# Attention heads on one core: squares, zero tests, row products and gate products move off VectorE

## The chip, the cores and the metric

The kernel runs on one core of a Trainium2 chip. The metric is the device time of one execution in microseconds, the median of three runs. The core's engines are TensorE (PE in the profile, its weight loads PEld), VectorE (DVE), ScalarE (ACT), GpSimd (POOL) and SyncE (SP), which only issues DMAs. All arithmetic that matters here is in float32.

## The reference

Two layers work on 3327 rows of 256 features, padded by the kernel to 3328, 26 tiles of 128 rows. Layer 0 is a graph layer and a mixture of eight experts; layer 1 is a graph attention layer and a block of attention heads. The change is in the last block alone, `_L1_ffn_ref`, which takes the normalized rows `x` and whose result is added to the rows:

```python
sx = einsum('bsh,ndh->bnsd', x, hl_w) + hl_b          # 4 heads n of 64 features d
pad = sx == 0
q = einsum('bnsd,neod->bneso', sx, wq)                # 4 queries e per head
k = einsum('bnsd,nod->bnso', sx, wk);  v = einsum('bnsd,nod->bnso', sx, wv)
att = softmax(einsum('bnesd,bntd->bnest', q, k) * d ** 0.5 + causal)
qkv = where(pad, 0.0, einsum('bnest,bntd->bnesd', att, v))
gs = softmax(einsum('bnsf,nef->bnse', out, gate_w) + gate_b)   # out: qkv with e and d side by side
mixed = sum over e of qkv * gs
hn = layernorm(mixed + sx, ln_g, ln_b)                # over the 64 features of each head, eps 1e-8
hx = relu(where(fx == 0, 0, fx @ fc1 + b1))           # fx: hn with the heads side by side
hx = layernorm(where(fx == 0, 0, hx @ fc2 + b2) + fx, fnorm_g, fnorm_b)
fg = softmax(fout @ fgate_w.T)                        # 4 gates, one per head
result = fout * fg
```

## The kernel before

`graph0`, `Experts.run` and `graph1` do the first three blocks in the first 985 us or so; `heads` does the last one and takes the rest. In `heads` every engine's instructions run in the order in which the Python code issues them: the helper `InOrder` ties each instruction to the one before it on the same engine, which is why the profile shows almost everything at line 61, and why groups are told apart by the names of their tiles.

The work of `heads` is cut into units, one for each tile `t` of 128 rows and each head `h`, and a unit into chunks of up to 512 earlier columns (`span`): a unit of tile `t` has `t // 4 + 1` chunks, 392 in all. For each chunk there is

- `fill` (TensorE): scores of four queries into four PSUM tiles `pqk`; the last chunk of a unit gets the causal mask by products with `own` and `after`;
- `drain` (VectorE): each of the four is copied to the SBUF tile `sc` and its row maximum taken; after the last chunk of a unit the maxima become `nmax` (`anmax` in the profile);
- `weigh` (ScalarE): four exponentials in place, with their sums in `den` (each followed by an accumulator read);
- `values` (SP's queue): four DMAs that bring the values `vr` from HBM;
- `turn` (VectorE): one transposition of `sc` in 32x32 blocks;
- `attend` (TensorE): products of `vr` and `sc`, added up in `po`.

At the end of a unit `over` copies `po` to `ot` (ScalarE) and multiplies it by `sxd`, which holds 1 where `sx` is not 0 (GpSimd); one iteration later `back` turns it through TensorE (`ptO`) and copies `qkv` and the gate products `glp` out. The loop over the chunks, with `k` the chunk of `attend`, issues drains a few chunks ahead (`wanted`), `attend(k)`, `turn(k + 1)`, values and half of the exponentials of chunk `k + 2`, `back`, `over`, one step of each open tail and preparation, the other half of the exponentials, and at most one `fill`. From tile 8 on the step of tails and preparations is left out in the iteration after a unit's end:

```python
if not ended or u["t"] < 8:
    run(tails)
    run(preps)
```

Two kinds of generators are stepped there, one step (up to the next `yield`) per iteration:

- `prepare(t)`, for the tile after the current one: a DMA brings `xres`; statistics (`pst`, `pmv`, `prs`); the normalized row `xn`; its transposition `xt`; `psxt` and from it `sxt`; four DMAs on SP's queue spread it to `sxd`, `v`, the keys `kt`, the queries `qt`; last `sxd` is compared with 0 and `sx` turned.
- `tail(t)`, once the four heads of a tile are there: the gates `gs` by `softmax4`, the mixture in `qkv` and `fx`, `norm4(fx)` (tiles `l1..`), the two linear layers (`ph`, `h`, `fo`), `norm4(fo)` (tiles `l2..`), the gates `fg` by `softmax4`, the last products and the DMA to the output. Up to three tails are open; `back` steps them until at most two are left before it adds one.

Copies out of PSUM that either engine can do go through `empty`, which keeps estimates of the work of ScalarE and VectorE in `load` and gives each copy to the engine that would be done first. It decides while the program is built. Each `load[...] +=` line of the diff below therefore also moves the copies that follow.

Of the kernel before, what the change touches and what calls it, by code (L numbers as in the profile page):

```python
# [12 lines left out]
F32 = mybir.dt.float32  # L13
# [13 lines left out]
D = 256  # L27
# [74 lines left out]
class Net:  # L102
# [670 lines left out]
    def heads(self, xs, vs, out):  # L773
        tc, a = self.tc, self.a
        nc = InOrder(tc)
        Q = 32
        with ExitStack() as ctx:
            one = ctx.enter_context(tc.tile_pool(name="at", bufs=1))
# [4 lines left out]
            sm = ctx.enter_context(tc.tile_pool(name="atsm", bufs=4))  # L783
# [7 lines left out]
            lng = self.load_rows(one, a["lng"][:64], 64, "lng")  # L791
            lnb = self.load_rows(one, a["lnb"][:64], 64, "lnb")
# [4 lines left out]
            fng = self.load_rows(one, a["fng"][:64], 64, "fng")  # L797
# [9 lines left out]
            for s in range(2):  # L807
                r = ds(64 * s, 64)
                for k in range(2):
# [3 lines left out]
                    for c in range(2):  # L813
                        self.nc.sync.dma_start(
                            out=wq[r, c, :, ts(k, 64)],
# [54 lines left out]
            def turned(src, dst):  # L870
# [3 lines left out]
                    nc.tensor.transpose(pt[:, k, :], src[:, ts(k, P)], self.ident)  # L874
                empty(dst, pt, D)

            def prepare(t, res):  # L880

                x = tl.tile([P, D], F32, tag="xres", name="xres", bufs=2)
                nc.sync.dma_start(out=x, in_=xs[ts(t, P), :])
                yield
                st = sm.tile([P, 6], F32, tag="pst", name="pst")
                mv = sm.tile([P, 2], F32, tag="pmv", name="pmv")
                rs = sm.tile([P, 1], F32, tag="prs", name="prs")
                nc.vector.bn_stats(st, x)
                nc.vector.bn_aggr(mv, st)
                nc.vector.tensor_scalar(rs, mv[:, 1:2], 1e-5, None, ALU.add)  # L890
                nc.gpsimd.tensor_tensor(rs, rs, self.nhalf[:, :1], ALU.pow)
                load["dve"] += 0.7
                yield
                xn = self.work.tile([P, D], F32, tag="xn", name="xn2", bufs=1)
                nc.vector.tensor_scalar(xn, x, mv[:, 0:1], rs, ALU.subtract, ALU.mult)
                load["dve"] += 0.35
                yield
                xt = self.work.tile([P, 2, P], F32, tag="xt", name="xt2")
                turned(xn, xt)
                yield  # L900
                pp = ps.tile([P, 2, P], F32, tag="b", name="psxt")
                for c in range(2):
                    for k in range(2):
                        nc.tensor.matmul(
                            pp[:, c, :], hlt[:, k, ts(c, P)], xt[:, k, :], start=(k == 0), stop=(k == 1)
                        )
                sxt = self.work.tile([P, 2, P], F32, tag="sxt", name="sxt")
                for c in range(2):
                    nc.scalar.activation(
                        sxt[:, c, :], pp[:, c, :], AF.Identity, bias=hlb[:, c : c + 1]  # L910
                    )
                load["act"] += 0.6
                yield

                sxd = self.work.tile([P, 4, P], F32, tag="sxd", name="sxd", bufs=3)
                for k in range(2):
                    for s in range(2):
                        nc.sync.dma_start(
                            out=sxd[ds(64 * k, 64), s::2, :], in_=sxt[ds(64 * s, 64), :, :]
                        )  # L920
                pp = ps.tile([P, 4, 64], F32, tag="b", name="pv")
                for c in range(2):
                    nc.tensor.matmul(
                        pp[:, 2 * c : 2 * c + 2, :], sxt[:, c, :], wv[:, c, :], start=True, stop=True
                    )
                v = self.work.tile([P, 4, 64], F32, tag="v", name="v", bufs=1)
                empty(v, pp, D)
                yield

                pp = [ps.tile([P, 2, P], F32, tag="b", name="pk") for _ in range(2)]  # L930
                for c in range(2):
                    for s in range(2):
# [12 lines left out]
                qt = tl.tile([P, 4, 2, P], F32, tag="qt", name="qt")  # L945
                pp = [ps.tile([P, 2, 2, P], F32, tag="b", name="pq") for _ in range(2)]
                for c in range(2):
                    for i in range(2):
                        for s in range(2):
                            r = ds(64 * s, 64)  # L950
                            nc.tensor.matmul(
                                pp[s][:, c, i, :], wq[r, c, i, :], sxt[r, c, :], start=True, stop=True
                            )

                for s in range(2):
                    empty(qt[:, s::2, :, :], pp[s], BLK, 8.0)
                yield
                nc.vector.tensor_scalar(sxd, sxd, 0.0, None, ALU.not_equal)
                load["dve"] += 0.4
                sx = tl.tile([P, D], F32, tag="sx", name="sx", bufs=5)  # L960
                turned(sxt.rearrange("p c q -> p (c q)"), sx.rearrange("p (c q) -> p c q", c=2))
                res.update(sx=sx, sxd=sxd, qt=qt)
# [80 lines left out]
            def turn(u, g):  # L1043
# [4 lines left out]
                nc.vector.transpose(w, w)  # L1048
                load["dve"] += 0.1 + 0.00417 * n


            po = ps_o.tile([P, 4, BLK], F32, tag="po", name="po")
            po = po[:, :, :P].rearrange("p q (e i) -> p q e i", e=4)
# [55 lines left out]
            def softmax4(g, n, tag):  # L1109

                g3 = g.rearrange("p (n e) -> p n e", e=4)
                m = sm.tile([P, n], F32, tag=tag + "m", name=tag + "m")
                s = sm.tile([P, 4 * n], F32, tag=tag + "s", name=tag + "s")
                s3 = s.rearrange("p (n e) -> p n e", e=4)
                nc.vector.tensor_reduce(m, g3, AX.X, ALU.max)
                nc.vector.tensor_tensor(s3, g3, m.unsqueeze(2).to_broadcast([P, n, 4]), ALU.subtract)
                yield
                nc.scalar.activation(s, s, AF.Exp)
                yield
                nc.vector.tensor_reduce(m, s3, AX.X, ALU.add)  # L1120
                nc.vector.reciprocal(m, m)
                nc.vector.tensor_tensor(s3, s3, m.unsqueeze(2).to_broadcast([P, n, 4]), ALU.mult)
                load["dve"] += 0.6
                load["act"] += 0.25
                return s

            def norm4(v, g, b, tag):

                mv = sm.tile([P, 4, 2], F32, tag=tag + "mv", name=tag + "mv")
                for h in range(4):  # L1130
                    st = sm.tile([P, 6], F32, tag=tag + "st", name=tag + "st")
                    nc.vector.bn_stats(st, v[:, ts(h, 64)])
                    nc.vector.bn_aggr(mv[:, h, :], st)
                rs = sm.tile([P, 4], F32, tag=tag + "rs", name=tag + "rs")
                nc.vector.tensor_scalar(
                    rs, mv.rearrange("p h s -> p s h")[:, 1, :], 1e-8, None, ALU.add
                )
                load["dve"] += 1.1
                nc.gpsimd.tensor_tensor(rs, rs, self.nhalf[:, :4], ALU.pow)
                v3 = v.rearrange("p (h d) -> p h d", h=4)  # L1140
                nc.gpsimd.tensor_tensor(v3, v3, mv[:, :, 0:1].to_broadcast([P, 4, 64]), ALU.subtract)
                nc.gpsimd.tensor_tensor(v3, v3, rs.unsqueeze(2).to_broadcast([P, 4, 64]), ALU.mult)
                nc.gpsimd.tensor_tensor(v3, v3, rows(g), ALU.mult)
                nc.gpsimd.tensor_tensor(v3, v3, rows(b), ALU.add)

            def tail(t, sx, qkv, glp, den):
# [13 lines left out]
                nc.vector.tensor_tensor(gl, gl, gb, ALU.add)  # L1160
                load["dve"] += 0.9
                gs = yield from softmax4(gl, 4, "gs")
                nc.vector.tensor_tensor(gs, gs, rd, ALU.mult)
                mx = qkv.rearrange("p h e d -> p (h e) d")
                nc.gpsimd.tensor_tensor(
                    mx, mx, gs.unsqueeze(2).to_broadcast([P, 16, 64]), ALU.mult
# [7 lines left out]
                nc.gpsimd.tensor_tensor(fx, fx, sx, ALU.add)  # L1174
                yield
                yield
                norm4(fx, lng, lnb, "l1")
                yield
                yield
                fxt = tl.tile([P, 2, P], F32, tag="fxt", name="fxt", bufs=2)  # L1180
# [22 lines left out]
                nc.gpsimd.tensor_tensor(fo, fo, fx, ALU.add)  # L1203
                yield
                yield
                norm4(fo, fng, fnb, "l2")
                yield
                yield
                fot = tl.tile([P, 2, P], F32, tag="fxt", name="fot", bufs=2)
# [640 lines left out]
```

## Time and profile before

| | |
|---|---|
| median of 3 runs | 3073.84 us (3071.78 to 3076.59) |
| the profiled execution | 3072.57 us, of which the span from first to last instruction 3070.9 us |
| mean TensorE clock granted | 0.965 |
| busy in the span: PE / DVE / ACT / POOL | 2704.3 / 2496.3 / 1676.9 / 888.8 us |
| VectorE: emptying `pqk` to `sc` | 1568 instructions, 897.6 us busy |
| VectorE: turning `sc` | 392 instructions, 816.0 us busy |
| ScalarE: exponentials in `sc`, with reads of their sums | 1568 pairs, 1041.2 and 302.9 us busy |
| GpSimd: `ot` times `sxd` | 104 instructions, 132.7 us busy |

An engine's busy time is the time in which at least one of its instructions runs; neighbouring instructions of an engine overlap a little, so the sum of durations is more than the time they take. A wait names the instruction whose end released the waiting one. The chain is found by going back from the last instruction, at each step to what released it, or to the instruction ahead of it on its engine.

### The profile page before, as it was taken

Reading aid. Unit: us, or ns where it says so; the run is one execution under the profiler, and the core shown is the slowest. Engines: PE = TensorE matmul, PEld = TensorE weight load, DVE = VectorE, ACT = ScalarE, POOL = GpSimd, SP = SyncE. Lnnn points to the kernel's source line nnn. Section 1 sums busy time; section 2 is a strip of 40 time slices with the busy share of each in tenths; the row PEclk is TensorE's granted clock in tenths of the full one; section 3 lists DMA queues with packets and bytes.
Section 4 is the critical chain, followed back from the end, with each engine's and each line's share of the span. In section 5 each row is a group of like instructions: output and inputs, shape, how many; then the busy total and the mean of one; then the engine's idle time right before and its main releaser. Section 6 shows DMA issues by size and latency. Waiting matters only on the chain.

```text
span 3070.9 us, 126719 instructions
## 1 busy us (share of the span) xinstructions
PE 2704.3 (88%) x54254; PEld 2009.7 (65%) x54254; DVE 2496.3 (81%) x6166; ACT 1676.9 (55%) x4566; POOL 888.8 (29%) x1208
## 2 busy tenths in 40 slices
PE   7999988788887888998999998899989999999884
PEld 5878878666776666666666666666656665666553
DVE  5103643799996678999999999999999999999994
ACT  6410145555553546666666665666656666565663
POOL 6431644711223254432232221222111211111112
PEclk9999999999998889999999999999999999999997
DMA  9994578566763223333333343333333333333431
GB/s 375 356 301 137 185 242 265 182 240 230 262 235 95 66 69 90 109 93 99 110 103 102 111 115 102 103 108 111 108 105 109 111 112 112 111 108 108 118 108 52
DMA packets 258193, 449.80 MB, mean 146 GB/s; under 512 B 58816, under 2 KB 156608, under 8 KB 257504
## 3 DMA queue, kind: packets, MB, share of 16 engines
q1 hardware_dynamic: 241232, 416.77, 44.3%
q0 software_dynamic: 6576, 18.02, 1.6%
q8 instruction: 428, 7.01, 1.0%
q10 hardware_dynamic: 9824, 6.91, 0.8%
q14 instruction: 133, 1.09, 0.1%
HBM read 393.37 MB, written 25.88 MB: 137 GB/s over the span
## 4 chain that ended last, share of the span: by engine, by line
DVE 44%; PE 21%; issue 3%; POOL 2%; ACT 1%; DMA 1%; SPq 0%; ACTq 0%; DVEq 0%; POOLq 0%
DVE sc L61 37%; PE po L61 7%; PE pqk L61 7%; PE acc L61 2%; PE ptO L61 2%; DVE l2mv L61 1%; PE pq L61 1%; DVE l1mv L61 1%; PE psxt L61 1%; DVE fo L61 0%; ACT sc L61 0%; DVE l2st L61 0%; DVE anmax L61 0%; DMA vr<-vs 0%; PE ph L61 0%
## 5 line engine op out<-in xcount | busy, mean ns | idle before, releaser
L61 ACT ACTIVATE sc<-sc,anmax 128x512 f32<-128x512 f32 (+3 forms) x1568 | 1041.2, 671 | 122.5 <-DVE anmax L61 122.3
L61 DVE TENSOR_SCALAR_CACHE_REDUCE sc<-pqk 128x512 f32<-128x512 f32 (+3 forms) x1568 | 897.6, 626 | 51.3 <-PE pqk L61 49.2
L61 PEld LDWEIGHTS po<-sc,vr 32*64 32x64 f32 x43728 | 667.6, 132 | 338.4 <-DVE sc L61 190.5
L61 PE MATMUL po<-sc,vr 32*64 32x128 f32 x43728 | 770.3, 277 | 120.9 <-DVE sc L61 70.4
L61 PE MATMUL pqk<-kt,qt 64*128 64x512 f32 (+3 forms) x3136 | 794.8, 579 | 42.5 <-DVE sc L61 16.9
L61 DVE STREAM_TRANSPOSE sc<-sc 128x2048 f32<-128x2048 f32 (+3 forms) x392 | 816.0, 2082 | 9.3 <-ACT sc L61 9.2
L61 PEld LDWEIGHTS pqk<-kt,qt 64*128 64x128 f32 x3136 | 312.5, 186 | 229.5 <-issue 80.5
L61 PE MATMUL acc<-wh,p 128*128 128x259 f32 x1352 | 309.9, 387 | 33.9 <-DVE p L61 33.9
L61 POOL TENSOR_TENSOR ot<-ot,sxd 128x512 f32<-128x512 f32 x104 | 132.7, 1276 | 658.3 <-ACT ot L61 628.5
L61 PEld LDWEIGHTS acc<-wh,p 128*128 128x128 f32 x1352 | 254.1, 190 | 92.1 <-DVE p L61 51.7
L61 PE MATMUL acc<-y,pan 128*128 128x256 f32 x1352 | 304.1, 385 | 11.1 <-DMA pan<-in_adjt_dram 9.4
L61 ACT ACTIVATION_READ_ACCUMULATOR sc<-sc,anmax 128x1 f32 x1568 | 302.9, 193 | 0.0
L61 PEld LDWEIGHTS acc<-y,pan 128*128 128x128 f32 x1352 | 258.3, 193 | 52.7 <-issue 17.1
L61 ACT ACTIVATE u<-u,d 128x512 f32<-128x512 f32 (+1 forms) x182 | 125.2, 688 | 158.7 <-DVE u L61 158.5
L61 ACT COPY qkv<-ptO 128x256 f32<-128x256 f32 x104 | 38.7, 372 | 226.4 <-PE ptO L61 226.4
L61 DVE SCALAR_TENSOR_TENSOR u<-bc,d 128x512 f32<-128x512 f32 (+1 forms) x182 | 135.3, 744 | 0.1
L61 PE MATMUL ptO<-igw,ot 128*128 128x68 f32 x832 | 116.7, 284 | 20.4 <-DVE sc L61 10.3
L61 DVE SCALAR_TENSOR_TENSOR p<-pan,u 128x512 f32<-128x512 f32 (+1 forms) x182 | 126.0, 692 | 10.6 <-PE acc L61 5.8
L61 PEld LDWEIGHTS ptO<-igw,ot 128*128 128x128 f32 x832 | 102.4, 194 | 39.5 <-issue 19.9
L61 DVE DVE_READ_ACCUMULATOR sc<-pqk 128x1 f32 x1568 | 128.2, 82 | 0.0
L61 ACT ACTIVATE junk<-ar 128x1664 bf16<-128x1664 f32 x52 | 82.7, 1591 | 65.3 <-DMA ar<-in_adj_dram 64.1
L61 PEld LDWEIGHTS <-own 64*128 64x128 bf16 x832 | 53.4, 94 | 92.9 <-issue 80.4
(286 smaller groups left out, 2868.0 us busy)
## 6 DMA issues: line engine op xcount, KB each, us to landing
vr<-vs SPq DMA_DIRECT2D x976, 128.0 KB
ar<-in_adj_dram SPq DMA_DIRECT2D x104, 832.0 KB
vr<-vs SPq DMA_DIRECT2D x544, 96.0 KB
pan<-in_adjt_dram SPq DMA_DIRECT2D x156, 256.0 KB
pan<-in_adjt_dram SPq DMA_DIRECT2D x26, 1024.0 KB
pan<-in_adjt_dram SPq DMA_DIRECT2D x20, 832.0 KB
w1e<-w SPq DMA_DIRECT2D x59, 256.0 KB
took<-places SPq DMA_DIRECT2D x59, 129.0 KB
```

What stands on the lines that cost most here:

```text
L61: made = make(*args, **kw)
```

## The change

It touches `heads` alone.

- **`norm4`**: instead of `bn_stats` and `bn_aggr` for each of four heads and an addition on VectorE, there is one sum over all four heads on VectorE (with the sign turned, `ns`), and four Square operations on ScalarE with the sum as bias, a scale of 64, and their sums in `rs`. GpSimd then scales `ns` and `rs` and goes on with power, shift and products as before. Two yields are new, so a norm takes three iterations instead of one.
- **`prepare`**: the normalized row `xn` is made by two GpSimd operations instead of one on VectorE, and the power before it is moved behind the yield, into the same step.
- **comparison with 0**: a new function `nonzero` takes Sign and then Square on ScalarE of the 256 columns of `sxt` into `nz`, and the four DMAs spread `nz` to `sxd`. The comparison of the 512 columns of `sxd` on VectorE is gone.
- **gates**: the last product of `softmax4` and the product of `gs` with `rd` are made by GpSimd.
- the estimates in `load` change with these.

```diff
@@ -874,6 +874,12 @@
                     nc.tensor.transpose(pt[:, k, :], src[:, ts(k, P)], self.ident)
                 empty(dst, pt, D)
+            def nonzero(dst, src):
+                nc.scalar.activation(dst, src, AF.Sign)
+                nc.scalar.activation(dst, dst, AF.Square)
+                load["act"] += 0.75
@@ -888,12 +894,12 @@
                 nc.vector.bn_stats(st, x)
                 nc.vector.bn_aggr(mv, st)
                 nc.vector.tensor_scalar(rs, mv[:, 1:2], 1e-5, None, ALU.add)
+                load["dve"] += 0.7
+                yield
                 nc.gpsimd.tensor_tensor(rs, rs, self.nhalf[:, :1], ALU.pow)
-                load["dve"] += 0.7
-                yield
                 xn = self.work.tile([P, D], F32, tag="xn", name="xn2", bufs=1)
-                nc.vector.tensor_scalar(xn, x, mv[:, 0:1], rs, ALU.subtract, ALU.mult)
-                load["dve"] += 0.35
+                nc.gpsimd.tensor_tensor(xn, x, mv[:, 0:1].to_broadcast([P, D]), ALU.subtract)
+                nc.gpsimd.tensor_tensor(xn, xn, rs.to_broadcast([P, D]), ALU.mult)
                 yield
                 xt = self.work.tile([P, 2, P], F32, tag="xt", name="xt2")
                 turned(xn, xt)
@@ -909,6 +915,8 @@
                     nc.scalar.activation(
                         sxt[:, c, :], pp[:, c, :], AF.Identity, bias=hlb[:, c : c + 1]
                     )
+                nz = self.work.tile([P, 2, P], F32, tag="nz", name="nz", bufs=1)
+                nonzero(nz, sxt)
                 load["act"] += 0.6
                 yield
@@ -916,7 +924,7 @@
                 for k in range(2):
                     for s in range(2):
                         nc.sync.dma_start(
-                            out=sxd[ds(64 * k, 64), s::2, :], in_=sxt[ds(64 * s, 64), :, :]
+                            out=sxd[ds(64 * k, 64), s::2, :], in_=nz[ds(64 * s, 64), :, :]
                         )
                 pp = ps.tile([P, 4, 64], F32, tag="b", name="pv")
                 for c in range(2):
@@ -955,8 +963,6 @@
                 for s in range(2):
                     empty(qt[:, s::2, :, :], pp[s], BLK, 8.0)
                 yield
-                nc.vector.tensor_scalar(sxd, sxd, 0.0, None, ALU.not_equal)
-                load["dve"] += 0.4
                 sx = tl.tile([P, D], F32, tag="sx", name="sx", bufs=5)
                 turned(sxt.rearrange("p c q -> p (c q)"), sx.rearrange("p (c q) -> p c q", c=2))
                 res.update(sx=sx, sxd=sxd, qt=qt)
@@ -1048,6 +1054,8 @@
                 nc.vector.transpose(w, w)
                 load["dve"] += 0.1 + 0.00417 * n
+            sq = one.tile([P, 64], F32, name="sq")
             po = ps_o.tile([P, 4, BLK], F32, tag="po", name="po")
             po = po[:, :, :P].rearrange("p q (e i) -> p q e i", e=4)
@@ -1119,26 +1127,31 @@
                 yield
                 nc.vector.tensor_reduce(m, s3, AX.X, ALU.add)
                 nc.vector.reciprocal(m, m)
-                nc.vector.tensor_tensor(s3, s3, m.unsqueeze(2).to_broadcast([P, n, 4]), ALU.mult)
-                load["dve"] += 0.6
+                nc.gpsimd.tensor_tensor(s3, s3, m.unsqueeze(2).to_broadcast([P, n, 4]), ALU.mult)
+                load["dve"] += 0.4
                 load["act"] += 0.25
                 return s
             def norm4(v, g, b, tag):
-                mv = sm.tile([P, 4, 2], F32, tag=tag + "mv", name=tag + "mv")
+                v3 = v.rearrange("p (h d) -> p h d", h=4)
+                ns = sm.tile([P, 4], F32, tag=tag + "ns", name=tag + "ns")
+                nc.vector.tensor_reduce(ns, v3, AX.X, ALU.add, negate=True)
+                load["dve"] += 0.35
+                yield
+                rs = sm.tile([P, 4], F32, tag=tag + "rs", name=tag + "rs")
                 for h in range(4):
-                    st = sm.tile([P, 6], F32, tag=tag + "st", name=tag + "st")
-                    nc.vector.bn_stats(st, v[:, ts(h, 64)])
-                    nc.vector.bn_aggr(mv[:, h, :], st)
-                rs = sm.tile([P, 4], F32, tag=tag + "rs", name=tag + "rs")
-                nc.vector.tensor_scalar(
-                    rs, mv.rearrange("p h s -> p s h")[:, 1, :], 1e-8, None, ALU.add
-                )
-                load["dve"] += 1.1
+                    nc.scalar.activation(
+                        sq, v[:, ts(h, 64)], AF.Square, bias=ns[:, h : h + 1], scale=64.0,
+                        accum_out=rs[:, h : h + 1],
+                    )
+                load["act"] += 1.2
+                yield
+                nc.gpsimd.tensor_scalar(ns, ns, 1 / 64, None, ALU.mult)
+                nc.gpsimd.tensor_scalar(rs, rs, 1 / 64**3, 1e-8, ALU.mult, ALU.add)
                 nc.gpsimd.tensor_tensor(rs, rs, self.nhalf[:, :4], ALU.pow)
-                v3 = v.rearrange("p (h d) -> p h d", h=4)
-                nc.gpsimd.tensor_tensor(v3, v3, mv[:, :, 0:1].to_broadcast([P, 4, 64]), ALU.subtract)
+                nc.gpsimd.tensor_tensor(v3, v3, ns.unsqueeze(2).to_broadcast([P, 4, 64]), ALU.add)
                 nc.gpsimd.tensor_tensor(v3, v3, rs.unsqueeze(2).to_broadcast([P, 4, 64]), ALU.mult)
                 nc.gpsimd.tensor_tensor(v3, v3, rows(g), ALU.mult)
                 nc.gpsimd.tensor_tensor(v3, v3, rows(b), ALU.add)
@@ -1160,7 +1173,7 @@
                 nc.vector.tensor_tensor(gl, gl, gb, ALU.add)
                 load["dve"] += 0.9
                 gs = yield from softmax4(gl, 4, "gs")
-                nc.vector.tensor_tensor(gs, gs, rd, ALU.mult)
+                nc.gpsimd.tensor_tensor(gs, gs, rd, ALU.mult)
                 mx = qkv.rearrange("p h e d -> p (h e) d")
                 nc.gpsimd.tensor_tensor(
                     mx, mx, gs.unsqueeze(2).to_broadcast([P, 16, 64]), ALU.mult
@@ -1174,7 +1187,7 @@
                 nc.gpsimd.tensor_tensor(fx, fx, sx, ALU.add)
                 yield
                 yield
-                norm4(fx, lng, lnb, "l1")
+                yield from norm4(fx, lng, lnb, "l1")
                 yield
                 yield
                 fxt = tl.tile([P, 2, P], F32, tag="fxt", name="fxt", bufs=2)
@@ -1203,7 +1216,7 @@
                 nc.gpsimd.tensor_tensor(fo, fo, fx, ALU.add)
                 yield
                 yield
-                norm4(fo, fng, fnb, "l2")
+                yield from norm4(fo, fng, fnb, "l2")
                 yield
                 yield
                 fot = tl.tile([P, 2, P], F32, tag="fxt", name="fot", bufs=2)
```

More of the change, by code (lines that the diff above doesn't have):

```diff
@@ L890, in prepare @@
                 nc.vector.tensor_scalar(rs, mv[:, 1:2], 1e-5, None, ALU.add)
-                nc.gpsimd.tensor_tensor(rs, rs, self.nhalf[:, :1], ALU.pow)
                 load["dve"] += 0.7
                 yield
+                nc.gpsimd.tensor_tensor(rs, rs, self.nhalf[:, :1], ALU.pow)
                 xn = self.work.tile([P, D], F32, tag="xn", name="xn2", bufs=1)
-                nc.vector.tensor_scalar(xn, x, mv[:, 0:1], rs, ALU.subtract, ALU.mult)
-                load["dve"] += 0.35
+                nc.gpsimd.tensor_tensor(xn, x, mv[:, 0:1].to_broadcast([P, D]), ALU.subtract)
+                nc.gpsimd.tensor_tensor(xn, xn, rs.to_broadcast([P, D]), ALU.mult)
                 yield
```

## The prediction, as put on record before the run

> **What bounds the kernel now.** I read the page's busy times first, then the stretches in order of time, the chain that ended last, and only then the groups, because a busy share over the whole span mixes stages. `heads` runs from about 985 us to the end. Busy times per engine (part 1 of the page), then three rows of the stretches (us; PE, PEld, DVE, ACT, POOL busy; clock; DMA):
>
> ```profile
> PE 2704.3 (88%) x54254; PEld 2009.7 (65%) x54254; DVE 2496.3 (81%) x6166; ACT 1676.9 (55%) x4566; POOL 888.8 (29%) x1208
> ```
>
> ```profile
> 985.00:1200.00 215.00, 171.62 (x3019) 132.99 (x3021) 145.63 (x489) 108.90 (x372) 87.37 (x100) 0.83 0.28 72
> 1200.00:3000.00 1800.00, 1639.00 (x45950) 1120.25 (x45953) 1731.46 (x4192) 1128.53 (x3366) 411.32 (x459) 0.99 0.38 107
> 3000.00:3071.00 71.00, 27.02 (x1036) 22.80 (x1019) 25.51 (x51) 22.70 (x67) 17.86 (x21) 0.71 0.18 50
> ```
>
> The 81% of VectorE hides a long stage in which it is 96% busy (1731 of 1800 us), and TensorE 91% (1639). Before 1200 us nothing is full: that stage hangs on latency, and so does the end. The chain over 1200 to 3000 us, and the waits there (who waited for whom: us, times, longest):
>
> ```profile
> by line: DVE sc L61 60.6%; PE po L61 11.2%; PE pqk L61 11.2%; issue 2.4%; PE ptO L61 1.9%; DVE l2mv L61 0.9%; DVE l1mv L61 0.8%; DVE fo L61 0.7%; DVE anmax L61 0.6%; PE pq L61 0.6%; DVE l2st L61 0.6%; PE psxt L61 0.6%; DVE l1st L61 0.5%; DV
> ```
>
> ```profile
> DVE sc L61 <- PE pqk L61: 38.9, 55, 3.1
> ...
> PE po L61 <- DVE sc L61: 68.6, 92, 1.5
> ```
>
> VectorE's emptying and turning of `sc` is 60.6% of the chain, and the norms (`l1st`, `l1mv`, `l2st`, `l2mv`) stand on it by name. VectorE waits 39 us for TensorE in 1800 us. So VectorE paces, with TensorE close behind: it idles 161 us.
>
> **What the Trainium skill says.** *SBUF — State Buffer*, "Who interferes with whom": GpSimd shares a port pair with VectorE, and contends with VectorE instructions that have two SBUF inputs or run in a two-port mode, not with others. The trace agrees for the two operations that fill VectorE (ns: least/median/most):
>
> ```profile
> L61 DVE TENSOR_SCALAR_CACHE_REDUCE sc<-pqk x1568: 252/682/692, 1000.3 to 2999.9; 128x512 f32<-128x512 f32 x104, 128x384 f32<-128x384 f32 x84, 128x256 f32<-128x256 f32 x6, 128x128 f32<-128x128 f32 x2
> ...
> L61 DVE STREAM_TRANSPOSE sc<-sc x392: 701/2301/2311, 1003.6 to 3021.6; 128x2048 f32<-128x2048 f32 x104, 128x1536 f32<-128x1536 f32 x84, 128x1024 f32<-128x1024 f32 x6, 128x512 f32<-128x512 f32 x2
> ```
>
> The most lies 10 ns over the median although GpSimd works a quarter of the time. More work on GpSimd thus costs these nothing. *ScalarE: Activation LUTs*, "What ACT_TABLE_LOAD costs": an ACTIVATE with a pointer operand takes 280 ns + 0.833 ns per element, and neighbours overlap by 93 ns; a switch of table set 2.66 us. The exponential of 512 would take 707 ns; the trace has 715. The changed program's instruction list has no table load more than the old one, so I price Sign and Square with none. *Perfetto Trace Analysis*, "GPSIMD Engine Instruction": a GpSimd duration is unreliable, time it by spacing; in the trace the 128x256 products stand 0.69 us apart at 0.61 us each.
>
> **The change part by part.** What VectorE loses, from its groups in `heads` (busy us, mean ns, then idle before):
>
> ```profile
> L61 DVE BATCH_NORM_STATS2 l1st<-fx 128x6 f32<-128x64 f32 x104 | 20.3, 195 | 6.0 <-POOL fx L61 6.0
> ...
> L61 DVE BATCH_NORM_AGGREGATE l2mv<-l2st 128x2 f32<-128x6 f32 x104 | 18.9, 182 | 3.6
> ...
> L61 DVE TENSOR_SCALAR xn<-xres,pmv,prs 128x256 f32<-128x256 f32 x26 | 12.5, 483 | 12.4 <-POOL prs L61 12.4
> ...
> L61 DVE TENSOR_SCALAR sxd<-sxd 128x512 f32<-128x512 f32 x26 | 11.2, 431 | 18.5 <-DMA sxd<-sxt 18.0 <-issue 0.4
> ```
>
> Busy times overlap, so I take spacing. In order of time one norm looks like this (start, us):
>
> ```profile
> 2565.01 0.18 DVE L61 BATCH_NORM_STATS2 l1st<-fx 128x6 f32<-128x64 f32 x1
> ...
> 2566.43 0.18 DVE L61 TENSOR_SCALAR l1rs<-l1mv 128x4 f32<-128x4 f32 x1
> 2566.53 0.67 DVE L61 TENSOR_SCALAR_CACHE_REDUCE sc<-pqk 128x512 f32<-128x512 f32 x1
> ```
>
> From 2565.01 to the next emptying at 2566.53 are 1.52 us for nine instructions. Spaced likewise: `xn` 0.33, comparison of `sxd` 0.36, the two gate products 0.39, the last product of `fg` 0.14. Per tile 2 x 1.52 + 0.33 + 0.36 + 0.39 + 0.14 = 4.26 us, over 26 tiles 111 us.
>
> What it gains: one sum 128x256 to 128x4 per norm. The trace has sums of 176 elements at 332 ns and 296 at 464: interpolated 0.42 us, spaced 0.36; at 52 of them 19 us. And the balance `load` shifts copies: by the instruction lists VectorE gets nine more (3 `kt`, 2 `v`, 2 `sx`, 1 `xt`, 1 `qt`), 8 x 0.36 + 0.63 = 3.5 us. Net 88 us off VectorE.
>
> What of it lies on the path: from 1200 to 3000 us about 21 tiles pass (86 `l2st` = 21.5 tiles, 19 `xn`), so about 89 us of the removed work is there. The pieces of the chain in that stretch, added up by name, give l2mv 15.3, l1mv 13.1, l2st 10.1, l1st 8.8, l2rs 8.0, l1rs 2.4, xn 7.2, sxd 6.6, and for `gss` and `fgs` (about half of their 11.9) 6.2: 77.7 us, 87% of it. The additions, 43 sums and most copies, 18.3 us, at the same 87% are 16. **62 us** net on the chain. The chain behind is TensorE's; a chunk of 512 costs it 4.0 us (in order of time around 2577 us: 1.92 for `pqk`, 2.05 for `po`), VectorE 4.75 (four emptyings 0.61 apart and a turn of 2.3); where an iteration also holds `psxt`, `pq` or `ptO` (1.1, 1.7, 1.05 us) TensorE takes over. I choose four fifths: 50. Bounds: 25 (two fifths) to 62.
>
> ScalarE gets 208 Squares of 64 with accumulator reads: 333 ns by the page, spaced 0.34 with the read of 193 ns (the 512 ones come 0.71 apart at 0.715 us), so 1.4 us per norm, 71 us, and 52 Sign/Square of 256, about 0.3 to 0.4 each, 18 us. It goes from 60% to some 65% of `heads` and stays below a chunk's pace (2.85 us of exponentials per 4.75). Behind a Square that waits stand the second half of the exponentials of the chunk two ahead and `ot`; the sum was issued one step earlier and VectorE is then past it. Cost 0 to 5 us, taken 0; the cover is that chunk of lead.
>
> GpSimd gets, per tile, two `xn` products (0.69 apart: 1.4 us), four small products on `ns` and `rs` (0.23 to 0.40 by the rows `deg` and `rs`: 1.3), three gate products (at least 0.20 by the row `dinv<-dinv,pos`: 0.8): 3.5 us, 91 us, 25% to 29% of `heads`. Three things queue there: `ot`, which `ptO` on TensorE waits for, the norm before `fxt`/`fot`, and `xn` before its transposes. By the list `xn` stands in a third of the tiles right behind `fo<-fo,fx`, whose input VectorE finishes after turning the next chunk (0.8 us), so 0.8 + 0.73 + 0.56 + 1.38 = 3.5 us after that turn, while TensorE reaches the transposes after its products, 2.05 us. 1.4 us late, in 8 tiles 11 us; TensorE's slack takes about half: cost 6. Bounds: 0 to 29 (every tile).
>
> The first tiles and the end: VectorE's waits of 18.0 us for the DMA of `sxd` (three times) and 12.4 us for `prs` are not its own any more; `ot` waits for that DMA now, which comes some 0.7 us later behind the two operations on `nz`. SP's queue holds the same four DMAs per tile. Most of these waits stand before the first chunk, where something else is late too: gain 6, bounds 0 to 20. The last tail is serial: per norm a sum 0.42, Squares 1.4, two small products 0.6 and handovers 0.2, 2.6 against 1.6 us, plus 0.5 for the gates: loss 3, bounds 2 to 6. The two new yields per norm lengthen a tail from 17 to 21 steps; three tails of at least 8 iterations each give 24, so from tile 8 nothing is forced; only tile 0's is, longer by four steps.
>
> Sum: 50 - 6 + 6 - 3 = 47 us off. The profiled execution took 3072.57 us (span 3070.9), 1.3 below the median of 3073.84: 3072.6 - 47 = 3025.6, shown as a median about **3026**.
>
> **Rivals.** *TensorE takes over*: for it speak 91% busy and the PE shares of the chain; against, VectorE waits only 39 us for it. Then two fifths of 62, less 6 and 3: 16 gained, about 3058; at the bounds of `xn` nothing, 3074. *GpSimd becomes the path* (slower): `xn` or `ot` comes late behind a norm, whose chain there is now 5 us. It decides from 50/21 = 2.4 us of TensorE stall per tile; one whole norm in the way is 21 x 5 = 105, 55 slower: 3129; at 3.3 us per tile about 3093. For it: `xn` has three GpSimd operations ahead of its transposes where it had one; against: `ptO` waited for `ot` under 27 us in all, and GpSimd idles 70%. *The change does not relieve VectorE*: the balance could hand copies back, but the lists show nine only. *ScalarE holds exponentials back*: 16 us of VectorE waits on it now; it would have to grow fivefold.
>
> **How the numbers follow.** Relief as worked out: 0.66, 2985 to 3050. TensorE takes over: 0.20, of which 0.05 within 0.2% (6 us, about what a measurement of this kernel tells from no change). GpSimd late 0.11, ScalarE 0.03: 0.14 slower. So 0.66 + 0.15 = 0.81 faster. Low end: 62 + 20 + 6 for sums that overlap more: 88 off, 2985; high end 3066, into the second case.
>
> **What would show it.** Right: `l1st`, `l1mv`, `xn`, `sxd` gone from VectorE, sums near 0.42 us, VectorE near 95% busy in the long stage with its waits for `pqk` up from 39 to 60 to 90 us, emptyings still 682 ns. Wrong: `pt` or `ptO` waiting for POOL `xn` or `ot` over 50 us; emptyings or turns longer; exponentials waiting; Squares far from 0.33 us.

## The result, and the profile after

The changed kernel takes 3045.44 us (median of 4 runs, 3040.98 to 3049.38) against 3074.34 us before: ratio 0.9906, 95% interval 0.9889 to 0.9923. It is faster by 29 us; 47 were forecast. The profiled execution of the changed kernel took 3049.38 us, with a span of 3047.7.

Busy time by engine, then the same three stretches as before (us; PE, PEld, DVE, ACT, POOL busy; clock; DMA share; GB/s):

```profile
PE 2699.4 (89%) x54254; PEld 2000.6 (66%) x54254; DVE 2408.8 (79%) x5629; ACT 1782.0 (58%) x5025; POOL 953.8 (31%) x1442
```

```profile
985.00:1200.00 215.00, 157.17 (x2536) 119.20 (x2543) 113.04 (x353) 106.27 (x377) 92.28 (x136) 0.77 0.25 62
1200.00:3000.00 1800.00, 1660.07 (x47263) 1136.12 (x47253) 1697.84 (x3822) 1252.43 (x3863) 476.77 (x663) 0.99 0.39 110
3000.00:3048.00 48.00, 10.21 (x223) 7.86 (x205) 5.03 (x19) 6.29 (x24) 16.75 (x25) 0.59 0.03 10
```

VectorE is busy 87.5 us less (2496.3 before). That is the relief that was worked out, 88, and yet the span is only 23 us shorter. In the first stretch fewer instructions pass in the same 215 us: 2536 of TensorE where there were 3019, and TensorE's own busy time falls. Something there takes longer.

The operations, from the groups in `heads` (busy us, mean ns, then idle before and its releaser). The first line is from the kernel before, all others are from the changed one:

```profile
L61 DVE TENSOR_SCALAR_CACHE_REDUCE sc<-pqk 128x512 f32<-128x512 f32 x976 | 613.0, 682 | 36.9 <-PE pqk L61 35.9
```

```profile
L61 DVE TENSOR_SCALAR_CACHE_REDUCE sc<-pqk 128x512 f32<-128x512 f32 x976 | 612.9, 682 | 51.4 <-PE pqk L61 49.7
L61 DVE TENSOR_REDUCE l1ns<-fx 128x4 f32<-128x256 f32 x26 | 10.2, 392 | 8.6 <-POOL fx L61 8.6
L61 DVE TENSOR_REDUCE l2ns<-fo 128x4 f32<-128x256 f32 x26 | 10.0, 383 | 15.0 <-POOL fo L61 15.0
```

```profile
L61 ACT ACTIVATE sq<-fx,l1ns 128x64 f32<-128x64 f32 x104 | 36.2, 349 | 9.7 <-DVE l1ns L61 7.2
L61 ACT ACTIVATION_READ_ACCUMULATOR sq<-fx,l1ns 128x1 f32 x104 | 19.6, 189 | 0.0
```

The sums take 0.39 us, the emptyings 682 ns as before: GpSimd's added work does not slow them. Ahead of them VectorE waits 49.7 us for `pqk`, where it waited 35.9.

To find the place, I cut `heads` at three events: the first `prs` on VectorE (its start), the last `ot` of tile 7 and the last `ot` of tile 25 on GpSimd. Their start times give three lengths (us); all later kernels are cut in the same way, each from one profiled execution:

```
                       first part   second part   end   ratio to before, 95% interval
                       tiles 0-7    tiles 8-25
before                   342.8       1714.3       37.3
changed                  370.1       1658.4       40.2   0.9906  0.9889-0.9923
early_old                340.0       1668.3       40.4   0.9822  0.9806-0.9838
norm_only                356.7       1683.0       39.9   0.9922  0.9898-0.9946
norm_old                 343.1       1707.6       37.6   0.9964  0.9952-0.9975
no_yield                 368.8       1759.8       40.2   1.0215  1.0195-1.0234
xn_old                   361.1       1661.8       40.1   0.9888  0.9856-0.9919
nz_old                   364.8       1656.4       40.1   0.9903  0.9875-0.9930
gates_old                364.6       1667.2       40.0   0.9891  0.9866-0.9917
norm_late                340.1       1660.4       39.5   0.9813  0.9788-0.9837
add_squares              353.3       1744.7       37.3   1.0089  1.0060-1.0119
add_products             352.0       1728.7       40.5   1.0068  1.0047-1.0089
from_4                   347.0       1658.2       40.1   0.9796  0.9774-0.9818
late_nz_old              340.2       1660.5       39.3   0.9817  0.9795-0.9840
```

From before to changed: the first part costs 27.3 us, the second gains 55.9, the end costs 2.9, and `heads` began 2.5 us later in this execution. Together 23.2, the difference of the spans. The change does what was hoped from tile 8 on and loses half of it again in the first eight tiles. Not all of the difference is waiting: for the same matmuls TensorE is busy 289.5 us in the first part, from 985 us on, against 281.7 before (granted clock 0.85 against 0.88), and 1531 against 1549 us in the second (1.00 against 0.99). Whether the clock follows the waits or comes by itself, these two executions do not tell. The chain of the first eight tiles, before (985 to 1319 us) and changed (985 to 1349 us):

```profile
by line: DVE sc L61 26.8%; PE pqk L61 12.9%; PE po L61 9.7%; issue 5.1%; PE ptO L61 4.8%; ACT sc L61 3.9%; PE psxt L61 2.1%; PE pq L61 2.0%; POOL fo L61 1.8%; PE pv L61 1.8%; PE pk L61 1.7%; PE pt L61 1.3%; DVE l1mv L61 1.3%; DVE l2mv L61 1
```

```profile
by line: PE pqk L61 14.9%; PE po L61 12.5%; ACT sc L61 6.7%; PE ptO L61 4.8%; issue 3.1%; ACT sq L61 2.7%; POOL fo L61 2.6%; DVE sc L61 2.0%; POOL fx L61 1.9%; POOL ot L61 1.4%; PE ph L61 1.4%; PE pq L61 1.3%; PE pt L61 1.3%; DMA vr<-vs 1.1
```

VectorE has all but left it: `sc` falls from 26.8% to 2.0%. In its place stand `sq` on ScalarE, exponentials, GpSimd's `fo`, `fx` and `ot`, and TensorE. A piece of the changed kernel's chain in order of time (start, us, what):

```profile
1126.62 1.26 POOL ot L61
...
1128.54 1.04 POOL l1rs L61
1129.58 0.59 POOL fx L61
...
1133.20 1.91 POOL qkv L61
...
1138.04 1.23 POOL ot L61
1139.32 1.99 PE ptO L61 x8
```

For 12.7 us one GpSimd operation follows another: a norm (from `l1ns` at 1127.96), the gates, the mixing of another tail, and only then `ot`, for which TensorE's `ptO` waits. Only about 1.2 us of these are work that is new on GpSimd (0.58 from `l1ns` to the power, 0.60 for the two gate products); the rest stood there before too. The piece shows where time is lost, and not how much of it the change adds. It looks like the slower rival of the prediction, "GpSimd becomes the path", in the first tiles alone, but it is not GpSimd by itself, as the experiments show.

### The profile page after: what moved, and what is told of

The parts are those of the page before. It is cut to its first block, busy times and chain, and to the rows that moved or that the text cites. A ratio compares the mean times of both kernels' runs of the same rounds, so it can differ in the third digit from the quotient of the medians.

```text
span 3047.7 us, 126910 instructions
## 1 busy us (share of the span) xinstructions
PE 2699.4 (89%) x54254; PEld 2000.6 (66%) x54254; DVE 2408.8 (79%) x5629; ACT 1782.0 (58%) x5025; POOL 953.8 (31%) x1442
## 4 chain that ended last, share of the span: by engine, by line
DVE 33%; PE 23%; ACT 4%; POOL 2%; issue 2%; DMA 0%; POOLq 0%; SPq 0%; ACTq 0%; DVEq 0%
DVE sc L61 30%; PE po L61 10%; PE pqk L61 9%; PE ptO L61 2%; ACT sc L61 2%; ACT sq L61 1%; POOL fo L61 1%; PE ph L61 1%; PE pt L61 0%; PE psxt L61 0%; PE pq L61 0%; POOL fx L61 0%; POOL ot L61 0%; POOL qkv L61 0%; DVE anmax L61 0%
## 5 line engine op out<-in xcount | busy, mean ns | idle before, releaser
L61 PEld LDWEIGHTS pqk<-kt,qt 64*128 64x128 f32 x3136 | 304.0, 188 | 208.6 <-issue 81.6
```

The lines of the kernel that those rows point to most:

```text
L61: made = make(*args, **kw)
```

## The experiments

The table above has the measured lengths. Times differ by chip: the kernel before ran at medians of 3074, 3085, 3080 and 3080 us beside the four groups of runs, so the ratios, each against the kernel before beside its own group, are the measure. The lengths are all set against the one profiled execution of the kernel before, from the first group; beside the other groups that kernel took 5 to 11 us more as a whole, and a difference of a few us between lengths of different groups says little.

**early_old** keeps the old operations in tiles 0 to 7. Each changed place asks for the tile:

```diff
-                yield from norm4(fx, lng, lnb, "l1")
+                yield from (norm4 if t >= 8 else norm4_old)(fx, lng, lnb, "l1")
-                nonzero(nz, sxt)
+                if t >= 8: nonzero(nz, sxt)
...
-                nc.gpsimd.tensor_tensor(gs, gs, rd, ALU.mult)
+                (nc.gpsimd if t >= 8 else nc.vector).tensor_tensor(gs, gs, rd, ALU.mult)
```

> Tiles 0 to 7 keep every step as before the change, tiles 8 to 25 have the changed steps. In the changed kernel tiles 0 to 7 took 30 us longer than before and tiles 8 to 25 took 56 us less. Theory A (in the short iterations of the first tiles the longer steps on GpSimd and ScalarE are on the path): the 30 us come back and the 56 stay, about 3018 us. Theory B (copies that the balance moves to VectorE wait there for TensorE): the copies stand as before here, so also about 3018. Theory C (the loss is no matter of the tile's place, or the gain of the late tiles is fed by the delay of the early ones): 3035 to 3045 us.

The first part takes 340.0 us, the second 1668.3, ratio 0.9822: 55 us faster than before on that chip, almost twice the gain of the changed kernel. The loss belongs to the tiles' place and can be had back; theory C falls. A and B both allow this.

**norm_only** is the kernel before with the changed `norm4` and its two calls, nothing else of the change; **norm_old** is the changed kernel with the `norm4` of before.

```diff
+                yield from norm4(fx, lng, lnb, "l1")      # norm_only: before, with this
-                yield from norm4(fx, lng, lnb, "l1")      # norm_old: changed, with the next
+                yield from norm4_old(fx, lng, lnb, "l1")
```

> Only the norms are changed; row products, comparison with 0 and gates stand as before, and so do nearly all copies (one qt more on VectorE). Theory A: a norm's steps are the longest, so 15 to 30 us of loss in tiles 0 to 7, and 2 x 1.16 of the 3.4 us per tile that VectorE is relieved of, two thirds of the 56 us, in the late tiles: 37; together 3055 to 3060 us. Theory B (moved copies): no loss in the first tiles, 3037 us.

> The norms stand as before; row products, comparison with 0 and gates are changed. The copies on VectorE are nearly those of the changed kernel (3 v, 6 kt, 3 qt, 2 sx). Theory A: at most 10 us of loss in tiles 0 to 7; a third of the gain in the late ones, 19; 3060 to 3066 us. Theory B: the loss of the first tiles stays at 25 to 30 us, so 3080 us.

Norms alone lose 13.9 us in the first part, everything but norms 0.3. So B, the moved copies, is out as the main cause: norm_old has those copies and no loss, norm_only has before's and a loss. In the second part norms gain 31 us and the rest 7, where A wanted 37 and 19. (In norm_only's profiled execution the TensorE clock was 0.95 and 0.94 in tiles 11 and 12, where early_old has 1.00, and these two took 10 us longer than there. This execution took 3065.01 us at a mean clock of 0.959, another of the same kernel 3053.61 at 0.966, so the 31 may be too few by about 10.) Norms and the rest together lose 13 us more in the first part than the two apart, and gain 18 more in the second, of which that clock may be 10.

**no_yield** takes the two new yields out of the changed norm, so that sum, squares and products are issued in one step:

```diff
                 nc.vector.tensor_reduce(ns, v3, AX.X, ALU.add, negate=True)
                 load["dve"] += 0.35
-                yield
...
                 load["act"] += 1.2
-                yield
```

> The changed kernel without the two new yields in the norm: sum, squares and GpSimd's part are issued in one step. If the early loss comes of the tail's four further steps, which are forced through for tile 0's tail: 10 to 20 us less in tiles 0 to 7. If it comes of the length of the operations: early tiles as in the changed kernel or slower, since ScalarE then waits in the same step for VectorE's sum. In the late tiles ScalarE's exponentials wait behind the squares: 0 to 20 us slower than the changed kernel. 3030 to 3065 us.

The first part as a whole stays at 368.8 us. That does not yet clear the four further steps of a tail, since a new wait may have taken the place of the old loss; the finer cut at the end of this section says more. The rest was a miss: 2.2% slower than before, not 0 to 20 us slower than the changed kernel. Its waits from 1350 to 3110 us (us in total, times, longest):

```profile
DVE sc L61 <- PE pqk L61: 117.5, 114, 4.2
...
ACT sq L61 <- DVE l1ns L61: 68.6, 18, 11.0
...
ACT sq L61 <- DVE l2ns L61: 37.9, 18, 5.8
DVE sc L61 <- ACT sc L61: 37.5, 35, 3.7
```

ScalarE stands 107 us at a Square whose sum VectorE has yet to make, half of its exponentials behind it, and VectorE waits 118 us for TensorE, against 46 in the changed kernel. TensorE is busy 1588 us there for the same matmuls, against 1531 in the changed kernel, at a granted clock of 0.97 against 1.00, so over half of the 101 us between the two shows as longer matmuls. The yields, which I had counted only as length, carry the gain.

**xn_old**, **nz_old** and **gates_old** are the changed kernel with one of the other three parts undone in all tiles:

```diff
-                nc.gpsimd.tensor_tensor(xn, x, mv[:, 0:1].to_broadcast([P, D]), ALU.subtract)
-                nc.gpsimd.tensor_tensor(xn, xn, rs.to_broadcast([P, D]), ALU.mult)
+                nc.vector.tensor_scalar(xn, x, mv[:, 0:1], rs, ALU.subtract, ALU.mult)   # xn_old
...
-                nonzero(nz, sxt)
+                nc.vector.tensor_scalar(sxd, sxd, 0.0, None, ALU.not_equal)              # nz_old
...
-                nc.gpsimd.tensor_tensor(gs, gs, rd, ALU.mult)
+                nc.vector.tensor_tensor(gs, gs, rd, ALU.mult)                            # gates_old
```

> The changed kernel with the normalized row xn made by VectorE as before. First stretch: from the first prs to tile 7's last ot the kernel before took 343 us, the changed one 370, norms alone 357, all but the norms 343. So 13 us come only of norms and the others together. Theory A1 (xn queues on GpSimd behind a norm and TensorE's transposes wait): 355 to 360 us there. Theory A2 (the gates do it, in the tail's own chain): 368 to 372. Second stretch, from there to tile 25's last ot (1714 before, 1658 changed): if xn on GpSimd is worth its 0.33 us of VectorE, 5 us more than changed, 1663; if its transposes wait for it, 1650 to 1657. Ratio to before: A1 0.986 to 0.988, A2 0.991.

> The changed kernel with the comparison with 0 made by VectorE on the 512 columns, as before. First stretch: A1 and A2 both expect 366 to 372 us (370 in the changed kernel); if instead the DMAs of v and vr that queue on SP behind the four that wait for nz cost time there, 360 us or less. Second stretch: 0.36 us per tile more on VectorE, 5 to 7 us, so 1664. Ratio to before 0.991 to 0.993, or 0.989 if the queue matters.

> The changed kernel with the three gate products made by VectorE as before. First stretch: A1 368 to 372 us, A2 (the gates lengthen the tail's chain on GpSimd) 355 to 362. Second stretch: 0.53 us per tile more on VectorE, 8 us, so 1666, unless GpSimd's gates come late behind norms. Ratio to before: A1 0.993, A2 0.989.

In the first part they give back 9.0, 5.3 and 5.5 us, so neither A1 nor A2 holds alone. The three sum to 20 where 13 were to be explained, and these are single executions, so the shares of the comparison and the gates are not settled; for `xn` the finer cut below shows the place. In the second part, in these single executions, `xn` on GpSimd is worth 3 us, the gates 9, the comparison nothing (undone, it is 2 us shorter). The ratios of the three and of the changed kernel overlap.

**norm_late** has the changed norms from tile 8 on and the other parts changed everywhere (`norm4 if t >= 8 else norm4_old`).

> The changed norms from tile 8 on alone; row products, comparison and gates changed in all tiles. Theory A (the early loss needs the changed norms): first stretch 342 to 348 us, second 1658 to 1668, ratio 0.982 to 0.985, as where tiles 0 to 7 kept all of it. If the first stretch stays over 355 us the others lose time by themselves there and the earlier run with old norms hid it.

340.1 and 1660.4 us, ratio 0.9813: as A expects, and a little better than its range. Taking the norms alone out of the first eight tiles gives back all that was lost. Some of the waits there, from 1002 to 1315 us:

```profile
DVE sc L61 <- PE pqk L61: 26.6, 21, 8.2
...
PEld pt L61 <- POOL xn L61: 9.7, 4, 4.3
...
PEld ptO L61 <- POOL ot L61: 8.9, 8, 4.5
```

and in the changed kernel from 1005 to 1349 us:

```profile
DVE sc L61 <- PE pqk L61: 33.2, 31, 3.9
...
PEld ptO L61 <- POOL ot L61: 14.3, 6, 6.3
DVE l2ns L61 <- POOL fo L61: 14.2, 3, 9.0
PEld pt L61 <- POOL xn L61: 12.8, 4, 4.9
```

The three that both lists show are longer in the changed kernel, and no single one explains 27 us.

**add_squares** and **add_products** ask which length of the norm it is. Both are the kernel before with filler and no relief: squares whose results nothing uses, and in each norm two products by 1 that its chain runs through.

```diff
+                js = sm.tile([P, 4], F32, tag="js", name="js")                           # add_squares
+                for h in range(4):
+                    nc.scalar.activation(sq, lng, AF.Square, bias=lnb[:, 0:1], scale=64.0,
+                                         accum_out=js[:, h : h + 1])
...
+                for _ in range(2):                                                       # add_products
+                    nc.gpsimd.tensor_tensor(v3, v3, rows(self.ones[:, :64]), ALU.mult)
```

> The kernel before, with four Squares of 64 columns added on ScalarE in each norm's step, on a constant tile and with sums that nobody reads: they take ScalarE's time (in the changed kernel 0.45 us apart, 1.8 us per norm) and nothing waits for them but what is queued behind. First stretch 343 us before, 357 with norms alone changed. Theory A3 (ScalarE's queue is held up in the short iterations): 350 to 357. Theory A4 (the tail's own chain sum, squares, GpSimd is longer): 343 to 346. Second stretch 1714 us before: 1714 to 1720 if ScalarE's 94 us more lie beside VectorE's work. Ratio to before: A3 1.003 to 1.005, A4 1.000 to 1.001.

> The kernel before, with two products by 1 added on GpSimd in each norm, in its chain: 1.5 us more from the statistics to the norm's result, about as much as the changed norm is longer by (sum 0.4, squares 1.8 and small products 0.6 in place of 1.5 us). First stretch: A4 355 to 362 us, A3 343 to 348. Second stretch 1714 to 1718, since a step has an iteration's time there. Ratio to before: A4 1.004 to 1.006, A3 1.000 to 1.002.

Both lose in the first part, 10.5 and 9.2 us, so a held-up ScalarE and a longer chain on GpSimd can each cost time there (A4 alone wanted 12 to 19). Whether this is the loss of the changed norm is another matter, to which the finer cut below says no for tiles 2 and 3. What neither expected is the second part, 30 and 14 us longer. By the timed ratios the squares cost 0.9% (0.6 to 1.2) and the products 0.7% (0.5 to 0.9). The filler squares on ScalarE:

```profile
L61 ACT ACTIVATE sq<-lng,lnb 128x64 f32<-128x64 f32 x208 | 72.3, 348 | 5.0
```

and the second part, before and with them (us; PE, PEld, DVE, ACT, POOL busy; clock; DMA), where ScalarE is busy 1134.53 of 1744 us:

```profile
1319.00:3033.00 1714.00, 1549.12 (x44298) 1059.84 (x44296) 1640.36 (x3905) 1075.63 (x3204) 363.08 (x404) 0.99 0.38 108
1333.00:3077.00 1744.00, 1570.87 (x44296) 1069.58 (x44293) 1640.57 (x3903) 1134.53 (x3498) 362.75 (x404) 0.98 0.37 106
```

VectorE's busy time there is before's, so it only waits: for `pqk` 67 us against 37. TensorE, with the same matmuls, is busy 22 us longer. Cut at each tile's last `ot`, nine of the eighteen tiles have a lower granted clock than before (0.92 to 0.99, where before has 0.97 to 1.00). They are 25 of the 30 us longer, and 22 us of that is TensorE's busy time; the other nine are 5 us longer. So most of what the squares cost here shows as longer matmuls at a lower clock. It was not one odd execution: the four timed runs had mean clocks of 0.957 to 0.960, the eight of the kernel before beside them 0.961 to 0.967. Why filler on ScalarE goes with a lower clock for TensorE was not tested. The products on GpSimd look alike: 12 of their 14 us are in five tiles with a lower clock.

**from_4** sets the limit of norm_late at tile 4; **late_nz_old** is norm_late with the comparison left on VectorE.

```diff
-                yield from (norm4 if t >= 8 else norm4_old)(fx, lng, lnb, "l1")
+                yield from (norm4 if t >= 4 else norm4_old)(fx, lng, lnb, "l1")      # from_4
```

> The changed norms from tile 4 on instead of tile 8, the rest changed in all tiles. If the early loss belongs to the tails forced through in the first four tiles' short loops: first stretch 340 to 348 us as with norms from tile 8 (340), second 1655 to 1660; ratio 0.980 to 0.982. If all of the first eight tiles lose with it: first stretch 350 to 356, ratio 0.983 to 0.986.

> Changed norms from tile 8 on, row products and gates changed in all tiles, comparison with 0 on VectorE in all tiles. With the comparison alone undone the second stretch was 2 us shorter and the first 5. So here: first stretch 337 to 342 us, second 1656 to 1664, ratio 0.979 to 0.982, the fastest version so far or level with it. If ScalarE's comparison is worth its 0.36 us of VectorE: second stretch 1666 to 1668, ratio 0.983 to 0.984.

from_4: 347.0 and 1658.2 us, ratio 0.9796, median 3019.20 us (3015.48 to 3021.94): of the 27 us lost all but 4 come of the tails of tiles 0 to 3. (This run and norm_late issue the same work up to tile 4. Their tiles 1 to 4 agree within 0.1 us and tile 0 differs by 2.7, which tells what a single execution is worth.) late_nz_old: 340.2 and 1660.5 us, ratio 0.9817, level with norm_late: the comparison on ScalarE brings nothing. The intervals of from_4, norm_late, late_nz_old and early_old overlap, so they are not told apart; all four are clear of the changed kernel's.

**The first part, cut finer.** With the last `ot` of tiles 1, 3 and 4 as further cuts, the same executions give (us):

```
                       tiles 0-1  tiles 2-3   tile 4    tiles 5-7
before                   78.7       65.1       59.0      140.0
changed                  82.1       76.9       64.3      146.9
norm_only                81.1       76.2       62.4      137.0
xn_old                   83.0       76.8       64.3      137.1
nz_old                   79.2       76.3       62.5      146.7
gates_old                81.5       76.4       61.7      145.0
no_yield                 83.5       70.5       64.8      149.9
add_squares              81.1       65.1       61.2      146.0
add_products             79.3       65.3       65.0      142.3
norm_old                 82.5       67.1       58.8      134.7
early_old                79.0       64.4       59.5      137.1
norm_late                79.7       66.6       58.7      135.2
from_4                   82.4       66.6       58.7      139.4
late_nz_old              80.1       67.1       58.6      134.4
```

The 27 us fall apart. In tiles 0 and 1 the 3.4 us are hardly more than what two executions of the same work differ by. In tiles 2 and 3 the five kernels that have the changed norms with their yields take 76 to 77 us, and the kernel before, those with the old norms and both fillers 64 to 67: longer work on one engine alone does not bring this loss (both fillers in one kernel were not run). Without the yields it is 70.5, so over half of it goes with them: a tail's four further steps, and with them the iteration that each step falls into, are part of the cause there. What the rest is stays open. In tile 4 the norms lose 3 to 6 us, and the fillers 2 and 6. In tiles 5 to 7 norms alone lose nothing, the changed kernel 7 us, and with `xn` back on VectorE it is 10 us shorter: there it takes the changed norms and `xn` on GpSimd together.

## Why the prediction was right, and where it was not

- **Direction and range**: faster, by 29 us where 47 were forecast, inside 2985 to 3066. The main term and its mechanism held. That the range also held the loss below is in part luck: its high end had been set for another rival, TensorE taking over.
- **What VectorE loses and gains**: 88 us net forecast, 87.5 measured as busy time. Sums 0.42 us forecast, 0.39 measured.
- **The long stage**: 50 less 6 forecast from 1200 us on. The `ot` that starts at 1200.4 us before starts at 1223.2 in the changed kernel; from there to the last `ot` the gain is 49 us, of 72 by which VectorE's busy time falls. So the 44 were nearly right. VectorE's wait for `pqk` in that stretch is 65.0 us against 42.7 (60 to 90 forecast; the 38.9 of the prediction leaves out the first 60 us of its stretch). But much of this rise belongs to tiles 5 to 7: from tile 8 on it is 45.7 against 36.8 us, while the gain there is 56 of 63 us of relief. The rival "TensorE takes over" in its strong form, two fifths, did not come.
- **`xn` late on GpSimd**: cost 6 forecast. With `xn` back on VectorE the second part is 3 us longer, in one execution: at most a small gain there, and a cost of about 10 us in tiles 5 to 7.
- **The end**: loss 3 forecast, 2.9 measured.
- **The first tiles**: this step failed. It forecast a gain of 6 us, bounds 0 to 20. Measured up to that same `ot` it is a loss of 20 us, over tiles 0 to 7 one of 27. I priced the waits that VectorE loses and did not price the norm's own lengthening there, though I had worked it out for the end (2.6 against 1.6 us), and I counted four forced steps of tile 0's tail and put them at nothing. The premise "that stage hangs on latency" was used only for what leaves VectorE. What the runs showed in its place: the loss needs the changed norms in the tails of the first tiles (norm_late, with none before tile 8, gives all 27 back; from_4, with none before tile 4, all but 4). In tiles 2 and 3, 12 us, over half goes with the two yields and none comes with filler on either engine; in tiles 5 to 7, 7 us, it takes `xn` on GpSimd too. How squares, GpSimd's chain, steps and clock share the rest stays open.
- **ScalarE**: "cost 0 to 5 us, taken 0". Filler squares cost 0.9%, about 27 us of timed run, in the kernel before, most of it at a lower granted clock. How much of it is paid in the changed kernel, where they are issued in another step, was not measured. The spacing was mis-sized as well: 0.34 us forecast, 0.47 in the trace. There each Square after the first starts 0.03 us after the accumulator read ahead of it has ended. In order of time:

```profile
1109.74 0.35 ACT L61 ACTIVATE sq<-fx,l1ns 128x64 f32<-128x64 f32 x1
1109.99 0.19 ACT L61 ACTIVATION_READ_ACCUMULATOR sq<-fx,l1ns 128x1 f32 x1
1110.21 0.35 ACT L61 ACTIVATE sq<-fx,l1ns 128x64 f32<-128x64 f32 x1
```

Four of them hold ScalarE 1.9 us, so 208 some 97 us instead of 71. The duration estimated from the Trainium skill, *ScalarE: Activation LUTs*, "What ACT_TABLE_LOAD costs", 333 ns, is near the measured 349. The overlap of 93 ns that the page gives for neighbouring ACTIVATEs is seen here from a Square to its read (0.10 us), and not from the read to the next Square.

## What to carry to other kernels

Price an edit in every stage of the loop, and by that stage's limit: here moving work off a full engine paid where it was full, and the same edit cost half of that again where the loop is short and hangs on latency. If the two stages are the same code, let the code ask for the tile. A step handed to another engine in an in-order queue needed its iteration of distance (without it the kernel was 2.2% slower than before), and the same distance is part of what costs time in the short loop. Cut the time by tile before naming a cause: filler that loses as many us may lose them in another place.

## What the runs showed of the hardware that was not expected

208 short ScalarE operations with unused results, 92 us of busy time with their reads on an engine that was busy 60% of `heads`, made the kernel before 0.9% slower (interval 0.6 to 1.2%). In the profiled execution 22 of the 30 us that the long stage grew by are TensorE's own busy time in tiles with a lower granted clock; why the clock fell is not shown. Squares of 64 columns with an accumulator come 0.47 us apart, exponentials of 512 with one 0.71, so the smaller operation costs far more than its share of columns.
